# Moving feed-forward tiles between the front and the steps of a scan

## The chip, the cores and the metric

The kernel runs on one core of a Trainium2 chip. The metric is device time in microseconds for one execution, the median of several runs. Its engines are called by the profile's names: PE (TensorE, matmuls), DVE (VectorE), ACT (ScalarE), POOL (GpSimd) and SP (SyncE, which here issues nearly all DMAs). Everything is float32.

## What is computed

The input x is 4 sequences of 1024 rows with 512 columns. A block of three layers is applied, each with a residual: half a feed-forward layer (ffn), a selective-scan (Mamba) layer, half a feed-forward layer with the same weights. Cut to what matters:

```python
x = x + 0.5 * ffn(layernorm(x))            # stage 1
x = x + mamba(layernorm(x))
x = x + 0.5 * ffn(layernorm(x))            # stage 2

def ffn(x):                                # inner size 1408
    g = (x @ gate_w.T) * gate_s
    u = (x @ up_w.T) * up_s
    return ((silu(g) * u) @ down_w.T) * down_s

def mamba(x):                              # inner size 1024, 16 states, conv of 4 taps
    h, gate = split(W_in @ x)
    h = silu(causal_conv(h) + conv_b)
    ts, Bm, Cm = rms parts of Wx @ h       # 128 + 16 + 16
    delta = softplus(Wdt @ ts + dt_bias)
    s_t = exp(delta_t * A) * s_(t-1) + delta_t * B_t * h_t     # along the sequence
    y = (sum over states of s_t * C_t) + D * h
    return Wout @ (y * silu(gate))
```

## The kernel before

Rows are cut into 32 tiles of 128. A scan step covers 256 rows (two tiles), so there are 16 steps, `NCS`, four for each sequence. Within a step the scan goes over 8 blocks of 128 inner channels and 4 groups of states: 32 units (`unit`, L553). A unit makes exps on ACT (L569), products on POOL (L572), four scans on DVE (L576), products with C on DVE (L584). Two units later, PE adds the states up with a small matmul into `yps` (L594).

Beside the units, other work is spread over the step as a list of parts. Each part has a cost for PE and for DVE, and the loop at the end of the kernel takes a part off whenever the units' share of the cost has run ahead (`done`, `vector`), or when the parts up to `ready[k]` have to be through in the first 22 of the 32 units. The parts of one step k are:

- `prep_*`: for step k+1, load x1 (`prep_load`, L336), normalize and transpose (`flips`, L645; `prep_flip`), the h half of W_in and the conv (`prep_conv`, `hp`, L372 and L383), the product with Wx (`sp`, L407), its transposes (`t`), and the DMAs that spread B and C (`bc`). The last of these parts is `ready[k]`.
- `gate(k)` (L534, `gp`): the gate half of W_in for step k itself. `tail(k - 1)` (L612, `op`): Wout of the step before.
- `FFN(k, tiles)` (L239): a group of feed-forward tiles that share one pass over the weights. `gate()` has 11 parts of 4 matmuls with as many columns as the group has rows, `up()` the same, `down()` has one part for each tile, 11 matmuls of 512 columns (`fo`, L315). After gate parts 3, 7 and 10 an ACT silu follows, between two loads of activation tables (L195, L196). A tile is (1, r) for stage 1 or (2, r) for stage 2. A step can prepare rows only after stage 1 of them is done, and stage 2 needs x2, written two steps later.

The 64 tiles (32 in each stage) are divided thus: the group `start` in front, one group beside each step, the group `end` behind. Before the change `start` has 2 tiles, step 0 has 4, step 1 has 2, steps 2 to 13 have 4, steps 14 and 15 have 2, the end has 4.

`front` is a hand-written list that runs before the first unit: `start`'s three products, then ffn[0]'s flips, step 0's preparation, and `BEGUN` = 7 of the 11 gate parts of ffn[0]. Then come the head of the first two and of the next two blocks (`head`, delta: `dp`, L486, with ACT, POOL) and their DMAs (`rows`, `spread`). Step 0's own list is written out separately in `background`: the last four gate parts and the up parts woven with `gate(0)`, then down, flips and conv for step 1, and `params` of step 1 at the very end.

Weights go through a ring of 14 buffers; a program-ordered queue loads at most `LEAD` = 12 blocks ahead, and the down blocks are held until a group's last down part. A part that is put off (`defer`) is emitted after the next part with a cost. The tile framework then gives each engine its own order; instructions that are pinned keep the program's. [...]

Of the kernel before, what the change touches and what calls it, by code (L numbers as in the profile page):

```python
# [23 lines left out]
J = T // P  # L24
CPB = L // T
NCS = B * CPB
# [5 lines left out]
HEAD = 10  # L32
BEHIND = 2
LEAD = 12
BEGUN = 7
RING = 14


@with_exitstack
def macaron_kernel(ctx: ExitStack, tc: tile.TileContext, a: dict, out: bass.AP):  # L40
# [119 lines left out]
    def settle():  # L160
        while deferred:
            deferred.pop(0)[1]()
# [18 lines left out]
    NOTHING = Work(0, 0, lambda: None)  # L181

    def then(f, *args):
        return Work(0, 0, lambda: f(*args))
# [54 lines left out]
    class FFN:  # L239
# [35 lines left out]
        def gate(self):  # L275
            self.done = 0

            def part(it):
                def emit(w):
                    if it == 0:  # L280
                        self.hd = p1.tile([P, NF, 2 * T], F32, tag="hd", name=f"hd{self.name}")
                    gp = self.product("gate_w", it, w[0])
                    nc.scalar.activation(  # L283
                        self.hd[:, it, : self.n], gp, AF.Copy, scale=gate_s[:, it : it + 1]
                    )
                    if it % 4 == 3 or it == NF - 1:
# [350 lines left out]
    def weave(xs, by):  # L637

        r = []
        for n, w in enumerate(xs):  # L640
            r.append(w)
            r += by[n : n + 1]
        return r, by[len(xs) :]

    def flips(f, prep):  # L645

        seq = [(f, t) for t in range(len(f.tiles))] if f else []
        if prep is not None:
            seq += [(None, j) for j in range(J)]
        xn = {}  # L650

        def begin(n):
            if n < len(seq):
                of, t = seq[n]
                xn[n] = of.stats(t) if of else prep_stats(prep, t)

        def start():
            begin(0)
            begin(1)

        def part(n):
            def emit():
                of, t = seq[n]
                if of:
                    of.flip(xn[n], t)
                else:
                    prep_flip(prep, t, xn[n])
                begin(n + 2)

            return Work(KH * P, H if n + 2 < len(seq) else 0, emit)  # L670

        return [Work(0, 2 * H, start)] + [part(n) for n in range(len(seq))]

    first = [(1, r) for r in range(J, NCS * J)]
    second = [(2, r) for r in range((NCS - 1) * J)]
    beside = {}
    for k in range(NCS):
        ones = min(len(first), 4 if k == 0 else 2)  # L680
        twos = 2 if k >= 2 else 0
        beside[k] = [first.pop(0) for _ in range(ones)] + [second.pop(0) for _ in range(twos)]
        assert NCS * J - len(first) >= min(NCS, k + 3) * J
        assert all(r < (k - 1) * J for stage, r in beside[k] if stage == 2)
    last = second + [(2, r) for r in range((NCS - 1) * J, NCS * J)]
    ffn = {k: FFN(k, beside[k]) for k in range(NCS)}

    def end_load():
# [5 lines left out]
    def background(k):  # L694

        f = ffn[k]
        if k == 0:
            down, turn, params = f.down(), flips(None, 1), prep_params(1)
            ready[k] = params[-1]
            return (  # L700
                weave(gate_0[BEGUN:] + f.up(), gate(0))[0] + down[:J]
                + [then(prep_load, 1), turn[0]] + weave(down[J:], turn[1:])[0] + [then(ffn[1].load)]
                + weave(prep_conv(1), flips(ffn[1], None))[0] + [NOTHING] + params
            )
        prep = k + 1 if k + 1 < NCS else None
        gates, out_of = gate(k), tail(k - 1)
        turn = flips(None, prep) if prep is not None else []
        conv = params = []
        if prep is not None:
            conv, params = prep_conv(prep), prep_params(prep)  # L710
            ready[k] = params[-1]
        parts = [then(tail_load, k - 1)]
        if prep is not None:
            parts.append(then(prep_load, k + 1))
        parts += turn[:1]
        p = [NOTHING] * 4 + gates + turn[1:] + out_of + conv
        tiles = f.gate() + f.up()
        p = [p[n : n + 2] for n in range(0, len(p), 2)]
        p += [[NOTHING]] * 4 + [[w] for w in params]
        turn = flips(ffn[k + 1], None) if k + 1 < NCS else []  # L720
        for n, w in enumerate(tiles):
            parts.append(w)
            for q in p[n : n + 1]:
                parts += q
            if n == len(tiles) - NF and k + 1 < NCS:
                parts.append(then(ffn[k + 1].load))
            if n == len(tiles) - NF and k + 1 == NCS:
                parts.append(then(tail_load, k))
                parts.append(then(end_load))
            if n == len(tiles) - 2:  # L730
                parts += turn[:1]
        w, turn = weave(turn[1:2] + f.down(), [NOTHING] + turn[2:])
        return parts + w + turn

    ready = {}


    start = FFN("p", [(1, r) for r in range(J)])
    down, gate_0 = start.down(), ffn[0].gate()
    turn_f, turn_m = flips(ffn[0], None), flips(None, 0)  # L740
    front = flips(start, None) + start.gate() + [then(load_resident)] + start.up()
    front += [down[0], turn_f[0], down[1], then(prep_load, 0)] + turn_f[1:] + [gate_0[0], gate_0[1]]
    front += [turn_m[0], gate_0[2]] + turn_m[1:] + prep_conv(0)
    front += weave(gate_0[3:BEGUN], prep_params(0))[0]
    beside_scan = [background(k) for k in range(NCS)]
    end = FFN("e", last)
    turn = flips(end, None)
    back_end = tail(NCS - 1) + turn + end.gate() + end.up() + end.down()
    for w in front + [w for b in beside_scan for w in b] + back_end:
        if w.blocks:  # L750
            queue.append(w)

# [4 lines left out]
    for w in front:  # L757
        do(w)
    settle()
    chores = head(0, 0)  # L760
    while chores:
        chores.pop(0)()
    for i in range(2):
        rows(0, i)
        spread(0, i)
    chores = head(0, 2)
    while chores:
        chores.pop(0)()
    units = NI * NS


# [122 lines left out]
```

## Time and profile before

| what | value |
|---|---|
| median of 3 runs | 3323.13 us (3322.13 to 3327.34) |
| profiled execution, its own time | 3324.85 us |
| its span | 3323.0 us |
| granted TensorE clock, mean | 0.975 |
| PE / DVE / ACT / POOL busy | 3129.9 / 2441.5 / 1877.0 / 1952.8 us |
| bytes moved by DMA | 506.42 MB, mean 152 GB/s |

The page gives busy time by engine, then 40 slices of 83 us with the busy share in tenths, then DMA, the chain of work that ended last, and the costliest groups. A waiting engine's idle time is put down to the instruction that released it last. Stages are not marked in the profile; they are found by counting scans (128 to a step).

### The profile page before, as it was taken

Reading aid. Unit: us, or ns where it says so; the run is one execution under the profiler, and the core shown is the slowest. Engines: PE = TensorE matmul, PEld = TensorE weight load, DVE = VectorE, ACT = ScalarE, POOL = GpSimd, SP = SyncE. Lnnn points to the kernel's source line nnn. Section 1 sums busy time; section 2 is a strip of 40 time slices with the busy share of each in tenths; the row PEclk is TensorE's granted clock in tenths of the full one; section 3 lists DMA queues with packets and bytes.
Section 4 is the critical chain, followed back from the end, with each engine's and each line's share of the span. In section 5 each row is a group of like instructions: output and inputs, shape, how many; then the busy total and the mean of one; then the engine's idle time right before and its main releaser. Section 6 shows DMA issues by size and latency. Waiting matters only on the chain.

```text
span 3323.0 us, 41725 instructions
## 1 busy us (share of the span) xinstructions
PE 3129.9 (94%) x12448; PEld 1615.6 (49%) x12448; DVE 2441.5 (73%) x4213; ACT 1877.0 (56%) x4300; POOL 1952.8 (59%) x1895
## 2 busy tenths in 40 slices
PE   8897688999999999999999999999999999988799
PEld 6534353545445444544545454454545454554434
DVE  2176697887778778787968778786877878698831
ACT  3445565746576564756556475665647465666430
POOL 1255667566666657567665756666575666667520
PEclk9988798999999999999999999999999999999899
DMA  7335466556466565545656555656555564556521
GB/s 238 109 92 136 124 175 169 159 135 180 124 171 168 169 168 144 161 132 172 162 161 174 146 156 131 185 149 172 161 159 157 133 187 128 173 166 171 165 92 45
DMA packets 287425, 506.42 MB, mean 152 GB/s; under 512 B 32096, under 2 KB 50272, under 8 KB 287200
## 3 DMA queue, kind: packets, MB, share of 16 engines
q1 hardware_dynamic: 285616, 503.31, 54.2%
q8 instruction: 100, 1.64, 0.2%
q14 instruction: 125, 1.02, 0.1%
q10 hardware_dynamic: 1584, 0.45, 0.1%
HBM read 442.03 MB, written 61.60 MB: 152 GB/s over the span
## 4 chain that ended last, share of the span: by engine, by line
PE 68%; DVE 18%; ACT 7%; POOL 3%; issue 3%; DMA 1%; SPq 0%; ACTq 0%; DVEq 0%; POOLq 0%
PE fo L315 15%; PE gate_w L269 13%; DVE da L576 10%; PE up_w L269 8%; PE gp L541 6%; PE yps L594 6%; PE op L623 6%; PE hp L372 5%; DVE pr L584 4%; ACT da L569 2%; PE dp L486 1%; DVE hd L300 1%; PE gate_we L269 1%; POOL sb L572 1%; PE foe L315 1%
## 5 line engine op out<-in xcount | busy, mean ns | idle before, releaser
L572 POOL TENSOR_TENSOR sb<-rep,bc 128x512 f32<-128x512 f32 x1024 | 1284.7, 1274 | 804.3 <-DVE da L576 639.8
L576 DVE TENSOR_TENSOR_SCAN da<-da,state,sb 128x256 f32<-128x256 f32 x1536 | 1049.7, 737 | 199.9 <-ACT da L569 161.1
L569 ACT ACTIVATE da<-rep,a_w 128x256 f32<-128x256 f32 x2048 | 902.2, 473 | 268.7 <-DVE pr L584 253.5
L584 DVE TENSOR_TENSOR pr<-da,bc 128x512 f32<-128x512 f32 x1024 | 660.2, 676 | 90.6 <-ACT state L581 81.1
L269 PE MATMUL gate_w<-fxT,w_gate_w 128*128 128x512 f32 (+1 forms) x1408 | 592.4, 566 | 8.4 <-ACT g L545 3.5
L269 PE MATMUL up_w<-fxT,w_up_w 128*128 128x512 f32 (+1 forms) x1408 | 577.4, 561 | 4.4 <-PE hp L372 3.4
L315 PE MATMUL fo<-w_down_w,hd 128*128 128x512 f32 x1276 | 563.5, 597 | 0.0
L594 PE MATMUL yps<-pr,fold 128*32 128x256 f32 x4096 | 370.4, 399 | 109.1 <-DVE pr L584 102.6
L269 PEld LDWEIGHTS gate_w<-fxT,w_gate_w 128*128 128x128 f32 x1408 | 266.6, 194 | 272.6 <-issue 233.9
L581 ACT COPY state<-da 128x2 f32<-128x2 f32 x768 | 120.2, 164 | 492.0 <-DVE da L576 483.3
L269 PEld LDWEIGHTS up_w<-fxT,w_up_w 128*128 128x128 f32 x1408 | 263.3, 192 | 271.5 <-issue 231.8
L315 PEld LDWEIGHTS fo<-w_down_w,hd 128*128 128x128 f32 x1276 | 239.8, 192 | 283.9 <-issue 278.8
L576 DVE TENSOR_TENSOR_SCAN da<-da,sb 128x256 f32<-128x256 f32 x512 | 321.7, 679 | 61.3 <-ACT da L569 48.1
L594 PEld LDWEIGHTS yps<-pr,fold 128*32 128x32 f32 x4096 | 108.6, 110 | 403.0 <-DVE pr L584 176.7
L372 PE MATMUL hp<-mxT,w_W_in 128*128 128x259 f32 x1024 | 241.2, 388 | 6.7 <-issue 2.5
L541 PE MATMUL gp<-mxT,w_W_in 128*128 128x256 f32 x1024 | 246.0, 388 | 0.8 <-ACT g L545 0.5
L623 PE MATMUL op<-w_Wout,u 128*128 128x512 f32 x512 | 230.7, 600 | 6.3 <-POOL sb L572 2.6
L517 POOL TENSOR_SCALAR e<-z 128x512 f32<-128x512 f32 x64 | 124.4, 1943 | 175.9 <-ACT z L498 167.6
L383 DVE SCALAR_TENSOR_TENSOR u<-hp,conv_w,u 128x256 f32<-128x256 f32 x384 | 176.2, 474 | 66.0 <-ACT u L376 61.0
L372 PEld LDWEIGHTS hp<-mxT,w_W_in 128*128 128x128 f32 x1024 | 190.8, 190 | 59.8 <-issue 21.0
L541 PEld LDWEIGHTS gp<-mxT,w_W_in 128*128 128x128 f32 x1024 | 188.3, 190 | 61.6 <-issue 22.9
L283 ACT ACTIVATE hd<-gate_w,gate_s 128x512 f32<-128x512 f32 (+1 forms) x176 | 113.9, 648 | 137.1 <-PE gate_w L269 136.9
(112 smaller groups left out, 2592.9 us busy)
## 6 DMA issues: line engine op xcount, KB each, us to landing
rep<-row SPq DMA_DIRECT2D x512, 256.0 KB, 5.4
w_W_in<-in_W_in_dram SPq DMA_DIRECT2D x256, 256.0 KB, 3.2
w_gate_w<-in_gate_w_dram SPq DMA_DIRECT2D x198, 256.0 KB, 4.0
w_up_w<-in_up_w_dram SPq DMA_DIRECT2D x198, 256.0 KB, 3.5
w_down_w<-down_w SPq DMA_DIRECT2D x187, 256.0 KB, 3.0
row<-dd SPq DMA_DIRECT2D x128, 256.0 KB, 3.0
w_Wout<-in_Wout_dram SPq DMA_DIRECT2D x128, 256.0 KB, 3.1
bc<-bcd SPq DMA_DIRECT2D x64, 256.0 KB, 5.3
```

The lines of the kernel that those rows point to most:

```text
L269: nc.tensor.matmul(o[:, : self.n], lhsT=w[:, k, :], rhs=self.xT[:, k, : self.n], start=(k == 0), stop=(k == KH - 1),)
L315: nc.tensor.matmul(op, lhsT=self.hd[:, it, t * P : (t + 1) * P], rhs=wd[it], start=(it == 0), stop=(it == NF - 1),)
L372: nc.tensor.matmul(hp[:, : K - 1 + T], lhsT=w[:, kk, :], rhs=st[k]["xnT"][:, kk, :], start=(kk == 0), stop=(kk == KH - 1),)
L383: pin(nc.vector.scalar_tensor_tensor(u[:, i, :], hp[:, q : q + T], conv_w[:, i, q : q + 1], u[:, i, :], ALU.mult, ALU.add,))
L517: lambda: pin(nc.gpsimd.tensor_scalar(e, z, 1.0, 1.0, ALU.add, ALU.subtract)),
L541: nc.tensor.matmul(gp[:, :T], lhsT=w[:, kk, :], rhs=st[k]["xnT"][:, kk, K - 1 :], start=(kk == 0), stop=(kk == KH - 1),)
L569: nc.scalar.activation(da[:, j, :], rep[:, h + j, 0, :], AF.Exp, scale=a_w[:, b0 + h + j, g : g + 1])
L572: nc.gpsimd.tensor_tensor(sb, rep[:, hs, 1, :], d["bc"][:, g : g + 1, :].to_broadcast([P, 2, T]), ALU.mult)
L576: nc.vector.tensor_tensor_scan(da[:, j, :], da[:, j, :], sb[:, j, :], 0.0 if first else state[:, b0 + h + j, g : g + 1], ALU.mult, ALU.add,)
L584: nc.vector.tensor_tensor(pr[:, hs, :], da, d["bc"][:, NS + g : NS + g + 1, :].to_broadcast([P, 2, T]), ALU.mult)
L594: nc.tensor.matmul(yp[j * Q : (j + 1) * Q, :], lhsT=fold, rhs=pr[:, j, :], start=(g == 0), stop=(g == NS - 1),)
L623: nc.tensor.matmul(op, lhsT=st[k]["u"][:, i, j * P : (j + 1) * P], rhs=wo[i], start=(i == 0), stop=(i == NI - 1),)
```

## The change

- `start` takes four stage-1 tiles in place of two. Its four down parts: two, then step 0's preparation begins (`prep_load(0)` and flips), the third down part and the fourth lie among them. ffn[0]'s flips are woven into the conv of step 0.
- ffn[0] has three tiles. Four of its gate parts (`FRONT`) lie in front, two between the first and the second head, five behind the second head.
- A table `BESIDE` gives each step's stage-1 and stage-2 tiles: steps 0, 1, 4, 7, 10, 13, 14 and 15 have three, steps 2, 3, 5, 6, 8, 9, 11 and 12 have four. The end keeps four.
- Step 0's list is built by the same code as the others' (without gate parts, Wout of an earlier step, and the four empty places in front): flips, `gate(0)`, conv and `params` for step 1 are woven with the up parts, and down comes last, with the flips of ffn[1].

```diff
-BEGUN = 7
+FRONT = 4
+BESIDE = [(3, 0), (3, 0), (2, 2), (2, 2), (1, 2), (2, 2), (2, 2), (2, 1), (2, 2), (2, 2), (2, 1), (2, 2), (2, 2), (1, 2), (0, 3), (0, 3)]
...
-    first = [(1, r) for r in range(J, NCS * J)]
-    second = [(2, r) for r in range((NCS - 1) * J)]
+    first = [(1, r) for r in range(2 * J, NCS * J)]
+    second = [(2, r) for r in range((NCS - 2) * J)]
...
-        ones = min(len(first), 4 if k == 0 else 2)
-        twos = 2 if k >= 2 else 0
+        ones, twos = BESIDE[k]
...
-    last = second + [(2, r) for r in range((NCS - 1) * J, NCS * J)]
+    last = [(2, r) for r in range((NCS - 2) * J, NCS * J)]
...
-        if k == 0:
-            down, turn, params = f.down(), flips(None, 1), prep_params(1)
-            ready[k] = params[-1]
-            return (
-                weave(gate_0[BEGUN:] + f.up(), gate(0))[0] + down[:J]
-                + [then(prep_load, 1), turn[0]] + weave(down[J:], turn[1:])[0] + [then(ffn[1].load)]
-                + weave(prep_conv(1), flips(ffn[1], None))[0] + [NOTHING] + params
-            )
...
-        parts = [then(tail_load, k - 1)]
+        parts = [then(tail_load, k - 1)] if k else []
...
-        p = [NOTHING] * 4 + gates + turn[1:] + out_of + conv
-        tiles = f.gate() + f.up()
+        p = [NOTHING] * (4 if k else 0) + gates + turn[1:] + out_of + conv
+        tiles = (f.gate() if k else []) + f.up()
...
+        for q in p[len(tiles):]:
+            parts += q
...
-    start = FFN("p", [(1, r) for r in range(J)])
+    start = FFN("p", [(1, r) for r in range(2 * J)])
...
-    front += [down[0], turn_f[0], down[1], then(prep_load, 0)] + turn_f[1:] + [gate_0[0], gate_0[1]]
-    front += [turn_m[0], gate_0[2]] + turn_m[1:] + prep_conv(0)
-    front += weave(gate_0[3:BEGUN], prep_params(0))[0]
+    front += [down[0], down[1], then(prep_load, 0), turn_m[0], down[2]] + turn_m[1:]
+    front += [turn_f[0]] + weave(prep_conv(0), [down[3]] + turn_f[1:])[0]
+    front += weave(gate_0[:FRONT], prep_params(0))[0]
...
+    between = gate_0[FRONT:]
...
+    for w in between[:2]:
+        do(w)
     chores = head(0, 2)
     while chores:
         chores.pop(0)()
+    for w in between[2:]:
+        do(w)
```

More of the change, by code (lines that the diff above doesn't have):

```diff
@@ L684, in macaron_kernel @@
         assert all(r < (k - 1) * J for stage, r in beside[k] if stage == 2)
-    last = second + [(2, r) for r in range((NCS - 1) * J, NCS * J)]
+    assert not first and not second
+    last = [(2, r) for r in range((NCS - 2) * J, NCS * J)]
     ffn = {k: FFN(k, beside[k]) for k in range(NCS)}
@@ L696, in background @@
         f = ffn[k]
-        if k == 0:
-            down, turn, params = f.down(), flips(None, 1), prep_params(1)
-            ready[k] = params[-1]
-            return (
-                weave(gate_0[BEGUN:] + f.up(), gate(0))[0] + down[:J]
-                + [then(prep_load, 1), turn[0]] + weave(down[J:], turn[1:])[0] + [then(ffn[1].load)]
-                + weave(prep_conv(1), flips(ffn[1], None))[0] + [NOTHING] + params
-            )
         prep = k + 1 if k + 1 < NCS else None
-        gates, out_of = gate(k), tail(k - 1)
+        gates, out_of = gate(k), tail(k - 1) if k else []
         turn = flips(None, prep) if prep is not None else []
@@ L748, in macaron_kernel @@
     back_end = tail(NCS - 1) + turn + end.gate() + end.up() + end.down()
-    for w in front + [w for b in beside_scan for w in b] + back_end:
+    for w in front + gate_0[FRONT:] + [w for b in beside_scan for w in b] + back_end:
         if w.blocks:
```

## The prediction

> **What bounds the kernel now.** I read the page from the top first. TensorE (PE) is the busy engine, in nearly every slice:
>
> ```profile
> PE 3129.9 (94%) x12448; PEld 1615.6 (49%) x12448; DVE 2441.5 (73%) x4213; ACT 1877.0 (56%) x4300; POOL 1952.8 (59%) x1895
> ...
> PE   8897688999999999999999999999999999988799
> ...
> PEclk9988798999999999999999999999999999999899
> ```
>
> The first slices and the ones near the end are the holes. So I cut the span into the stages of the program. A step makes 128 scans, so every 128th scan is a border: first scans at 169.7, 371.8, 547.3 and so on. The view by windows (length, then busy us of PE, PEld, DVE, ACT, POOL, then the clock):
>
> ```profile
> 0.00:169.70 169.70, 143.77 (x509) 96.07 (x510) 35.83 (x79) 67.97 (x104) 30.78 (x53) 0.97 0.57 174
> 169.70:371.80 202.10, 162.97 (x661) 84.68 (x659) 144.59 (x255) 101.34 (x267) 106.68 (x101) 0.89 0.43 115
> 371.80:547.30 175.50, 135.66 (x620) 76.01 (x620) 148.56 (x260) 104.56 (x268) 124.68 (x121) 0.87 0.56 160
> 547.30:740.50 193.20, 187.23 (x715) 93.62 (x716) 151.49 (x261) 115.54 (x276) 122.03 (x119) 0.98 0.54 146
> 931.10:1119.60 188.50, 187.00 (x752) 93.88 (x751) 146.37 (x263) 116.32 (x281) 123.67 (x120) 1.00 0.57 157
> 1119.60:1314.60 195.00, 192.18 (x763) 96.16 (x762) 153.51 (x262) 117.54 (x283) 121.01 (x117) 1.00 0.57 160
> 2847.90:3029.90 182.00, 157.95 (x764) 95.69 (x763) 147.20 (x257) 112.89 (x286) 121.34 (x114) 0.93 0.64 182
> 3029.90:3188.70 158.80, 134.88 (x576) 71.14 (x574) 131.87 (x217) 82.07 (x168) 101.37 (x86) 0.92 0.51 151
> ```
>
> Rows in order: front, steps 0, 1, 2, 4, 5, 14, 15. Steps 2 to 13 carry four feed-forward tiles each, take 188.5 to 195.0 us (mean 191.9), and PE lacks only 1.5 to 6 us: they are PE-bound. Steps 1, 14 and 15 carry two tiles and PE idles 24 to 40 us, but they last 175.5, 182.0 and 158.8 (step 15 prepares no next step). They are held by VectorE (DVE) and what it waits for: length minus DVE busy is 27.0, 34.8 and 26.9, mean 29.6. In PE-bound steps the same difference is about 40 (195.0 - 153.5 = 41.5; 188.5 - 146.4 = 42.1).
>
> What a tile costs on PE is read where PE runs undisturbed, in the chain in order of time (88 records are 44 matmuls, two records each):
>
> ```profile
> 12.00 21.32 PE gate_wp L269 x88
> 33.33 18.99 PE up_wp L269 x88
> 52.32 18.88 PE fop L315 x44
> ...
> 3243.69 37.77 PE up_we L269 x88
> 3281.45 37.78 PE foe L315 x88
> ```
>
> A matmul of 512 columns takes 37.77/44 = 0.858 us, one of 256 takes 18.99/44 = 0.43: time goes with columns. One tile (128 columns in 88 gate and up matmuls, 11 down matmuls of 512) is 88 x 0.2145 + 11 x 0.858 = 28.3 us, in whatever group it sits. Before and after there are 18 groups (front, 16 steps, end), so weight loads, silu calls and DMA bytes stay; nothing is saved by size. A four-tile step needs 189 us of PE, a three-tile one 161, a two-tile one 132.
>
> **Front: +31 us.** Tiles 2 to 4, so 56.6 us more PE. But ffn[0] shrinks from four tiles to three, and its eleven gate parts, all before the first scan in both orders, go from 11 x 3.55 (39 us) to 11 x 2.6 (28.6). Step by step: two more normalized tiles ahead of the first matmul cost about 2 (ACT 0.81 + 0.58 each, partly overlapped), so it starts at 14. Gate, up and down of four tiles at end-stage prices are 38.5 + 38.2 + 37.8 = 114.5 (the 256-column gate of before ran at 0.485 instead of 0.43, and that loss goes). Then flips of the next step 2.2, hp 14.3 (before's own 89.67 to 103.8), three ffn[0] flips 2, the wait for silu of u 5.5, sp + gate part + sp 7.2, two gate parts 5.2, transposes to dp about 2: 38.4, so dp at 167, where before had it at 134.85. The silu wait was 8.5 because a silu of hd stood ahead of u's on ACT; the new order puts u's first.
>
> From dp to the first scan before took 34.8, and it ended on PE, not on the rep transfer:
>
> ```profile
> 134.85 1.97 PE L486 MATMUL dp<-tsT,w_dt 128*128 128x256 f32 x8 [0.61 <-DVE tsT L451]
> 169.00 0.75 DVE L300 SCALAR_TENSOR_TENSOR hd<-up_w,up_s,hd 128x512 f32<-128x512 f32 x1 [4.41 <-PE up_w L269]
> 169.67 1.27 DVE L576 TENSOR_TENSOR_SCAN da<-da,sb 128x256 f32<-128x256 f32 x2
> ```
>
> DVE's scan stood behind an hd multiply that waited for up_w. The new order keeps that: ahead of the first scan PE has two dp, seven gate parts, two up parts and three gp: 1.8 + 18.2 + 5.2 + 5.3 = 30.5, and ACT has the third gp copy and then the exps, about 1. With PE stalls of 2.4, as before at 143.12 and 149.78: 167 + 34 = 201. SP issues row and rep of tiles 0 and 1 ahead of later weights, so they land in the shadow of this. Two new waits in the front: fo of the fourth tile holds the eleven down blocks of 14 ring buffers, so W_in loads for hp 3 on follow it (3.2 us to land; they start 9 us earlier: nothing); hp 1 waits for it on PE (counted). First scan at 201, +31.3; I allow +27 to +40.
>
> **Step 0: -28 us.** 202.1 is DVE 144.6 and 57.5 idle. What goes: the 9.9 us wait at the border for bc of step 1; most of 15.0 us in which DVE waited for fo; 2.9 for xi (windowed timeline, 250.64 and 252.50), since x1 rows 2 and 3 now come from the front; about 2 of hd.
>
> ```profile
> POOL sb L572 <- DMA bc<-bcd: 20.1, 1, 20.1
> DVE xf L323 <- PE fo L315: 15.0, 4, 6.2
> DVE da L576 <- POOL sb L572: 11.8, 3, 9.9
> ```
>
> The bc chain was last in step 0; the new order emits conv and params before down, and PE's order shows sp and t beside units 4 and 5 of 8. PE has only 28 (up) + 28 (down) + 59 (gp, hp, yps, sp, dp, flips) = 115 us, no bound. DVE 143 (nine hd multiplies 0.16 shorter, one xf less, one stats more) + idle 57.5 - 26.8 = 30.7: 173.7. The xf waits shrink to about 3: two-tile steps show none.
>
> **Three-tile steps: the term that decides.** DVE busy is known: 3.4 less than in a four-tile step (11 hd multiplies at 0.58 for 0.745, one xf 0.68, one stats 0.85), 2.8 more than with two tiles. Its idle is not shown for three tiles. It lies between 29.6 (two) and 40 (four). PE needs 161 of some 182, so it stops being the bound and I take the value nearer to two tiles: 32.5, and keep 25.4 (step 1 less its 1.6 of bc wait) and 40 for the range. What is late next is ACT: the three hd silus, g's and u's block the exps (a table load 1.28, the silu, a load 1.28), and step 14 shows two such waits of 7.2 and 9.2 us at two tiles.
> - Steps 4, 7, 10, 13 lose a tile: 188.5, 191.0, 192.9, 193.5 become 143.0, 150.3, 149.8, 148.6 plus 32.5: 175.5, 182.8, 182.3, 181.1. Together -44.2.
> - Step 1 gains one: 150.4 + 32.5 = 182.9, +7.4 (its start no longer carries stalled work done early in step 0).
> - Step 14: 150.0 + 32.5 = 182.5, +0.5.
> - Step 15: 133.9 + 29.5 = 163.4, +4.6; PE needs 138.
>
> Four-tile steps keep their length: step 2 follows a step with spare PE and still took 193.2. The end, the same four tiles, keeps 134.3. SP sees the same blocks; xi of a next step asks for at most the same store as before, and in steps 1 to 13 for one row earlier, so no queue is moved past a later store.
>
> **Sum:** +31.3 - 28.4 - 44.2 + 7.4 + 0.5 + 4.6 = -28.8. The profiled execution has span 3323.0 and its own time 3324.85, the median is 3323.13, so I subtract from the median: 3294.
>
> [...] In two-tile steps the granted clock falls: 0.87, 0.93, 0.92 against 1.00. The change puts some PE idle into four more steps. [...] At 0.93, PE's 161 become 173, still under 182; at 0.87 they become 185, 2.5 us over, about 15 in six steps. [...] I take 0.93, as three tiles leave fewer gaps than two.
>
> **Rivals.**
> 1. Slower: the three-tile step stays at the pace of a four-tile one, because ACT, PE and DVE wait for each other in turn (PE's yps for pr, ACT's hd for gate_w, DVE's scan for the exp). For: four-tile idle 40 while step 14 has 34.8 with half the tiles. Against: step 15 has 26.9 and step 1 27.0. Price: idle 40 adds 7.5 x 6 = 45, so 3339. It decides from an idle of 32.5 + 28.8/6 = 37.3 on.
> 2. Better: DVE idle as in step 1, 25.4, since PE is no longer asked for all its time: -43, 3251.
> 3. The change doesn't shorten step 0: DVE waits for fo as before (15) because flips, fo and yps interleave, or the front ends at +40. Either alone +9 to +12: 3304; with idle at 36 it is no change.
>
> **How the numbers follow.** Less than a 0.2% change (6.6 us) is about what a measurement of this kernel can't tell from none. Main case, idle 29 to 36: 0.47, of it 0.45 faster, 0.02 same. Rival 2: 0.15, faster. Rival 1: 0.25, slower mostly, 0.03 same. Rival 3 with idle near 36: 0.13, of it 0.02 faster, 0.08 same, 0.03 slower. So faster 0.62, same 0.13, slower 0.25. Range: rival 2's 3251 and rival 1's 3339 are its ends, rounded to 3254 and 3340, with 2 in 10 outside.
>
> **What would show it.** After the change: first scan near 201; no bc wait at the step 0 to 1 border; step 0 near 174; steps 1, 4, 7, 10, 13, 14 at 176 to 183 with DVE idle about 32; PEclk there above 0.93. Three-tile steps over 187, or a first scan past 210, would prove it wrong.

## The result, and the profile after

The changed kernel takes 3304.23 us, the median of four runs (3302.43 to 3307.95); the kernel before took 3324.42 beside it. The ratio is 0.9941 with an interval of 0.9926 to 0.9956: about 20 us faster. The forecast was 3294, so the sign is right, the range holds the time, and about a third of the forecast gain is missing. The profiled execution of the changed kernel is its slowest of the four, 3307.95 with a span of 3306.2; stage sums below are made against that span, which is 16.8 shorter than the 3323.0 of before.

The first part of the page, and the rows of PE and of its clock in 40 slices:

```profile
PE 3139.3 (95%) x12448; PEld 1612.0 (49%) x12448; DVE 2435.9 (74%) x4213; ACT 1879.9 (57%) x4299; POOL 1949.8 (59%) x1895
...
PE   8988898999999999999989999999999999999999
...
PEclk9988999999999999999999999999999999999999
```

The totals hardly move, as they should: the same work was put elsewhere. The hole near the end of before (slices 36 to 38) is gone; what is left of the first hole is mostly step 0. The view by windows, cut again at every 128th scan; columns are bounds and length, busy time of PE, PEld, DVE, ACT and POOL, then clock, DMA share and GB/s:

```profile
0.00:199.90 199.90, 183.44 (x536) 98.73 (x536) 40.99 (x83) 69.33 (x101) 31.77 (x56) 1.00 0.46 140
199.90:368.20 168.30, 134.30 (x579) 70.97 (x580) 139.41 (x254) 96.71 (x261) 112.64 (x107) 0.86 0.50 141
368.20:556.90 188.70, 171.06 (x726) 90.93 (x724) 151.39 (x262) 115.27 (x282) 120.16 (x118) 0.97 0.59 162
556.90:750.40 193.50, 187.43 (x714) 93.60 (x715) 151.69 (x260) 115.75 (x276) 121.31 (x119) 0.98 0.51 142
940.40:1122.20 181.80, 173.31 (x780) 94.81 (x778) 144.89 (x264) 117.14 (x290) 122.38 (x118) 0.98 0.65 180
1122.20:1314.60 192.40, 186.42 (x714) 93.31 (x715) 151.61 (x260) 115.50 (x276) 120.05 (x118) 0.98 0.53 146
2820.60:3008.80 188.20, 173.25 (x732) 92.16 (x731) 150.17 (x260) 115.19 (x282) 120.59 (x116) 0.96 0.58 159
3008.80:3171.30 162.50, 154.24 (x596) 72.91 (x595) 133.67 (x219) 82.31 (x164) 100.99 (x86) 0.97 0.51 150
```

These are the front and steps 0, 1, 2, 4, 5, 14 and 15, as before. All stages, in us:

| stage | before | forecast | after | change forecast | change measured |
|---|---|---|---|---|---|
| front | 169.7 | 201 | 199.9 | +31.3 | +30.2 |
| step 0 | 202.1 | 173.7 | 168.3 | -28.4 | -33.8 |
| step 1 | 175.5 | 182.9 | 188.7 | +7.4 | +13.3 |
| steps 4, 7, 10, 13 | 765.9 | 721.7 | 737.3 | -44.2 | -28.6 |
| step 14 | 182.0 | 182.5 | 188.2 | +0.5 | +6.2 |
| step 15 | 158.8 | 163.4 | 162.5 | +4.6 | +3.7 |
| eight steps of four tiles | 1534.7 | as before | 1526.4 | 0 | -8.3 |
| end | 134.3 | 134.3 | 134.9 | 0 | +0.6 |
| sum | 3323.0 | | 3306.2 | -28.8 | -16.7 |

The last column adds to 16.7 and the spans differ by 16.8; that is rounding.

What the front's four tiles cost on PE is read from the chain in order of time, whose rows are start, length and group:

```profile
14.76 40.80 PE gate_wp L271 x88
55.56 37.77 PE up_wp L271 x88
93.32 28.32 PE fop L317 x66
...
125.29 9.44 PE fop L317 x22
```

Gate, up and down take 40.8 + 37.8 + 37.8 = 116.3 against 114.5 forecast: at four tiles the front runs at the price of the end stage (37.8 each), except that the gate took 3.0 more, of which 0.7 were forecast. The timeline of the front's end (start, length, instruction, and in brackets the idle time before it and what ended that):

```profile
167.81 1.10 PE L488 MATMUL dp<-tsT,w_dt 128*128 128x256 f32 x4 [0.61 <-DVE tsT L453]
196.49 0.62 DVE L302 SCALAR_TENSOR_TENSOR hd<-up_w,up_s,hd 128x384 f32<-128x384 f32 x1 [5.35 <-PE up_w L271]
199.87 2.44 DVE L578 TENSOR_TENSOR_SCAN da<-da,sb 128x256 f32<-128x256 f32 x4 [2.76 <-ACT da L571]
```

dp comes at 167.8 (167 forecast) and the first scan at 199.9 (201). Only the last releaser is another one: the scan waited 2.76 for ACT's exp, not for the hd multiply before it, which was done 2.8 earlier.

The view of waits in step 0 (who waited for whom, us in all, times, longest) has no wait for bc any more, and none of DVE for fo:

```profile
DVE u L602 <- PE yps L596: 10.7, 3, 8.3
POOL sb L574 <- DVE xf L325: 7.3, 1, 7.3
DVE pr L586 <- ACT state L583: 6.8, 11, 2.6
...
DVE da L578 <- ACT da L571: 4.6, 3, 2.8
```

Before, DVE lost 15.0 to fo and POOL 20.1 to bc, 9.9 of which DVE lost again. DVE's idle time, length less busy, falls from 57.5 to 28.9. In step 7, which carries three tiles, the same view shows what DVE waits for now:

```profile
DVE da L578 <- ACT da L571: 15.4, 7, 4.1
DVE u L602 <- PE yps L596: 12.1, 4, 5.5
...
DVE hd L302 <- PE up_w L271: 4.3, 3, 3.3
```

Before, with four tiles, the first lines of the same step were these:

```profile
DVE da L576 <- ACT da L569: 17.6, 8, 6.5
DVE xf L323 <- PE fo L315: 8.9, 2, 7.1
DVE u L600 <- PE yps L594: 4.4, 4, 2.0
```

The exps are the largest item, before and after, and no item holds the 36.0 us of idle alone. With one tile less the wait for fo is gone; in its place came longer waits for yps and for up_w, which are results of PE too. DVE idle in the six three-tile steps is 37.3, 36.9, 36.0, 32.8, 32.0 and 38.0 (steps 1, 4, 7, 10, 13, 14), mean 35.5.

### The profile page after: what moved, and what is told of

Read it like the earlier page. It is cut to its first block, busy times and chain, and to the rows that moved or that the text cites. A ratio compares the mean times of both kernels' runs of the same rounds, so it can differ in the third digit from the quotient of the medians.

```text
span 3306.2 us, 41606 instructions
## 1 busy us (share of the span) xinstructions
PE 3139.3 (95%) x12448; PEld 1612.0 (49%) x12448; DVE 2435.9 (74%) x4213; ACT 1879.9 (57%) x4299; POOL 1949.8 (59%) x1895
## 4 chain that ended last, share of the span: by engine, by line
PE 66%; DVE 19%; ACT 8%; issue 3%; POOL 2%; DMA 1%; SPq 0%; DVEq 0%; ACTq 0%; POOLq 0%
PE fo L317 13%; PE gate_w L271 13%; DVE da L578 11%; PE up_w L271 8%; PE gp L543 6%; PE yps L596 6%; PE op L625 5%; PE hp L374 4%; DVE pr L586 4%; ACT da L571 2%; PE dp L488 1%; DVE u L385 1%; PE gate_wp L271 1%; PE gate_we L271 1%; PE foe L317 1%
## 5 line engine op out<-in xcount | busy, mean ns | idle before, releaser
L571 ACT ACTIVATE da<-rep,a_w 128x256 f32<-128x256 f32 x2048 | 906.9, 475 | 296.5 <-DVE pr L586 280.5
L271 PE MATMUL gate_w<-fxT,w_gate_w 128*128 128x384 f32 (+1 forms) x1408 | 579.4, 558 | 17.4 <-ACT hd L285 12.2
L271 PE MATMUL up_w<-fxT,w_up_w 128*128 128x384 f32 (+1 forms) x1408 | 564.0, 549 | 6.3 <-PE hp L374 2.3
L317 PE MATMUL fo<-w_down_w,hd 128*128 128x512 f32 x1232 | 544.3, 595 | 3.0 <-ACT fxT L236 3.0
L317 PEld LDWEIGHTS fo<-w_down_w,hd 128*128 128x128 f32 x1232 | 228.8, 190 | 276.3 <-issue 267.0
L543 PEld LDWEIGHTS gp<-mxT,w_W_in 128*128 128x128 f32 x1024 | 188.3, 191 | 67.6 <-issue 20.2
L374 PEld LDWEIGHTS hp<-mxT,w_W_in 128*128 128x128 f32 x1024 | 191.3, 191 | 58.9 <-issue 18.0
L285 ACT ACTIVATE hd<-gate_w,gate_s 128x384 f32<-128x384 f32 (+1 forms) x176 | 111.5, 636 | 97.9 <-PE gate_w L271 97.2
```

The costliest lines, as they stand in the source:

```text
L271: nc.tensor.matmul(o[:, : self.n], lhsT=w[:, k, :], rhs=self.xT[:, k, : self.n], start=(k == 0), stop=(k == KH - 1),)
L317: nc.tensor.matmul(op, lhsT=self.hd[:, it, t * P : (t + 1) * P], rhs=wd[it], start=(it == 0), stop=(it == NF - 1),)
L374: nc.tensor.matmul(hp[:, : K - 1 + T], lhsT=w[:, kk, :], rhs=st[k]["xnT"][:, kk, :], start=(kk == 0), stop=(kk == KH - 1),)
L543: nc.tensor.matmul(gp[:, :T], lhsT=w[:, kk, :], rhs=st[k]["xnT"][:, kk, K - 1 :], start=(kk == 0), stop=(kk == KH - 1),)
L571: nc.scalar.activation(da[:, j, :], rep[:, h + j, 0, :], AF.Exp, scale=a_w[:, b0 + h + j, g : g + 1])
```

## The experiments

Two questions were open. Which part of the change brings the gain: the order of step 0 or the spreading of tiles? And what holds a three-tile step at 185.7 (the mean of the six) when PE has been relieved of a tile? For the second there were several accounts, and from "Two tiles where there are three" on the expectations letter them. One is the prediction's own: ACT's silus, and the table loads around them, keep the exps back, and PE is no bound (A). Against it stand PE itself (B), the wait of u for yps (C), ACT's state copies (E), and no single engine at all, but a chain through DVE and the short exchanges between engines (D). In the first three experiments A is another theory, spelled out there.

One caution goes for all of them: an edit of one line lets the framework plan a new order of instructions on every engine, and steps change by a few us with it: in the run with two tiles, of the steps that keep theirs, step 14 changed by -6.0 and the eight four-tile steps by -3.0 to +1.6. A difference of 2 or 3 us in one step shows little; one of 10 or more, or one of the same sign in all six steps, can be read. Except where another kernel is named, edits are to the changed kernel.

### Step 0 in its old order

```diff
+        if k == 0:
+            down, turn, params = f.down(), flips(None, 1), prep_params(1)
+            ready[k] = params[-1]
+            woven, rest = weave(down[J:], turn[1:])
+            return (
+                weave(f.up(), gate(0))[0] + down[:J]
+                + [then(prep_load, 1), turn[0]] + woven + rest + [then(ffn[1].load)]
+                + weave(prep_conv(1), flips(ffn[1], None))[0] + [NOTHING] + params
+            )
```

> The changed kernel with one part undone: step 0's list in its old order (up woven with gate, then down, then flips, conv and params for step 1 last), front and distribution as changed. Theory A (the order of step 0 is what paid for the front): step 0 goes from 168 to about 190 and the wait for bc at its end comes back (about 10 us), so about +25 us, 3329, or no gain left. Rival (step 0 is short only because it has less matmul work): step 0 stays below 173, within 5 us of the changed kernel's 3304.

Measured: 3323.09 us, ratio to the kernel before 0.9999 (0.999 to 1.0007). The whole gain is gone. Its step 0 by windows:

```profile
198.50:386.80 188.30, 146.21 (x649) 81.53 (x650) 139.73 (x254) 106.10 (x273) 107.63 (x104) 0.88 0.47 134
```

and two of the waits in it:

```profile
POOL sb L574 <- DMA bc<-bcd: 13.8, 1, 13.8
...
DVE hd L302 <- PE up_w L271: 13.0, 4, 4.5
```

Step 0 is 188.3 instead of 168.3 at the same DVE work (139.7 and 139.4): 20 us more of DVE idle, and the bc wait is back. So the order is worth 20 of step 0's 33.8; the other 14 (202.1 - 188.3) come with what moved to the front. But the order has to be paid for: step 0 can only be ordered like the others because x1 rows 2 and 3 come from the front.

### The spread alone, in the kernel before

```diff
+BESIDE = [(4, 0), (3, 0), (2, 2), (2, 2), (1, 2), (2, 2), (2, 2), (2, 1), (2, 2), (2, 2), (2, 1), (2, 2), (2, 2), (2, 2), (0, 3), (0, 3)]
...
-        ones = min(len(first), 4 if k == 0 else 2)
-        twos = 2 if k >= 2 else 0
+        ones, twos = BESIDE[k]
```

> The kernel before with the distribution alone: front of two tiles and step 0 of four as before, then three tiles in steps 1, 4, 7, 10, 14, 15, four in the others. Theory A (a three-tile step takes 182 to 189, hardly less than a four-tile step, and 6 to 13 more than a two-tile one): what steps 4, 7, 10 and the steps after them save (18 to 25 us), steps 1, 14, 15 pay back (about 20), so 3318 to 3324. Rival (evening out is the gain): -15 us or more, below 3309.

Measured: 3314.52 us, ratio 0.9971 (0.996 to 0.9982), 9 us faster than before, half of what the whole change brings. The windows of steps 0 and 1:

```profile
168.80:376.00 207.20, 168.71 (x665) 86.24 (x663) 143.92 (x257) 106.03 (x271) 107.77 (x104) 0.90 0.41 112
376.00:562.50 186.50, 154.79 (x642) 78.36 (x642) 151.30 (x260) 106.72 (x268) 125.22 (x121) 0.89 0.56 156
```

Step 0, which this edit leaves at four tiles in the old order, took 5 more than before, and step 1 pays 11 for its third tile, step 15 3.7, step 14 nothing (182.0); steps 4, 7 and 10 fall to 180.7, 188.0 and 184.6, by 7.8, 3.0 and 8.3. Both theories missed: the rival wanted under 3309, the other 3318 or more.

### Front and order alone, no spread

```diff
-BESIDE = [(3, 0), (3, 0), (2, 2), (2, 2), (1, 2), (2, 2), (2, 2), (2, 1), (2, 2), (2, 2), (2, 1), (2, 2), (2, 2), (1, 2), (0, 3), (0, 3)]
+BESIDE = [(4, 0), (2, 0), (2, 2), (2, 2), (2, 2), (2, 2), (2, 2), (2, 2), (2, 2), (2, 2), (2, 2), (2, 2), (2, 2), (0, 2), (0, 2), (0, 2)]
```

> The changed kernel with the distribution uneven again: front of four and step 0 in the new order, step 0 with four tiles, step 1 with two, steps 2 to 12 with four, 13 to 15 with two. Theory A (even or uneven matters little): steps 4, 7, 10, 11 get 6 us each longer, steps 1, 13, 14, 15 shorter by 5 to 10 each, step 0 some 5 longer: 3300 to 3312. Rival (evening out is the gain): 3320 or more.

Measured: 3330.2 us, ratio 1.0017 (1.001 to 1.0024): slower than before, and 26 slower than the changed kernel. Theory A had not expected that; the rival, 3320 or more, came true. Steps 0 and 1:

```profile
203.30:378.80 175.50, 148.92 (x614) 73.84 (x613) 140.86 (x254) 95.96 (x261) 111.75 (x104) 0.93 0.47 133
378.80:564.90 186.10, 155.25 (x704) 93.57 (x702) 148.50 (x261) 114.76 (x284) 120.74 (x119) 0.88 0.58 163
```

Two things are to be seen. Step 0 in the new order with four tiles takes 175.5: 26.6 less than before, which does not pay for a front of 203.3 (+33.6). And step 1 with two tiles takes 186.1, where before's took 175.5 with two, at the same DVE work (148.5). So the idle of 27.0, on which the prediction rested, belongs to that one step of before. A possible reason lies in the traces: there a part of step 1's gate products had been done in step 0. The gate products of the feed-forward group by window (length, PE busy and records, then clock, DMA share and GB/s), in steps 0, 1 and 14 of before:

```profile
169.70:371.80 202.10, 12.09 (x40) 0.89 0.43 115
371.80:547.30 175.50, 14.24 (x48) 0.87 0.56 160
2847.90:3029.90 182.00, 26.77 (x102) 0.93 0.64 182
```

A group's gate has 88 records; before's step 1 did 48 of them, this kernel's 80. ACT has 104.6 us of work in the one and 114.8 in the other. Whether this is all of the difference in idle was not tested.

Set beside the changed kernel, these spans tell the price of a tile by place. A third tile on top of two costs 2.6 in step 1, 3.1 in 13, 4.0 in 14, 3.7 in 15. A fourth taken away saves 7.2 in step 0, 6.7 in 4, 3.0 in 7, 8.1 in 10. The front is 3.4 shorter, because ffn[0] is smaller by a tile. That is 13.4 paid and 28.4 saved, 15.0 of the 22.1 us between the two spans; 5.0 more come in step 11, which keeps its four tiles, and the rest is smaller than the changes of order.

So front and order alone cost 6, the spread alone brings 9, and both bring 20. They don't add. With the new front and the spread but the old order, the front uses up all that the spread brings (the first experiment, 3323); with front and order but no spread, the kernel is slower than before. The spread pays alone; the front and the order pay only together, and beside the spread.

### Two tiles where there are three

```diff
-BESIDE = [(3, 0), (3, 0), (2, 2), (2, 2), (1, 2), (2, 2), (2, 2), (2, 1), (2, 2), (2, 2), (2, 1), (2, 2), (2, 2), (1, 2), (0, 3), (0, 3)]
+BESIDE = [(3, 0), (3, 0), (2, 2), (2, 2), (1, 1), (2, 2), (2, 2), (2, 0), (2, 2), (2, 2), (2, 0), (2, 2), (2, 2), (1, 1), (0, 3), (0, 3)]
...
+    more_end = FFN("x", second)
+    back_end += [then(more_end.load)] + flips(more_end, None) + more_end.gate() + more_end.up() + more_end.down()
```

The four tiles taken out make a second group at the end, so only the steps are read, not the total.

> The changed kernel with only two tiles in steps 4, 7, 10 and 13; the four tiles left over go into a second group of four behind the end (about 115 us more there). Read are the lengths of the four steps, 181.7, 188.0, 184.6 and 183.0 in the changed kernel (mean 184.3). Theory A (the length is VectorE's busy time plus ScalarE's table loads and silus, which are the same for two and three tiles): only VectorE's 2.8 us less, mean 181. Rival B (the load of TensorE still sets the waits): the 28 us less of matmuls take 8 us or more off, mean 176 or less. Total 3405 or 3389.

Measured: 3413.09 us in one run. Steps 4, 7, 10, 13 take 180.1, 175.7, 184.8 and 183.5, mean 181.0, against 184.3. Steps 7 and 10 by windows:

```profile
1503.40:1679.10 175.70, 154.02 (x758) 92.84 (x756) 148.92 (x261) 106.34 (x224) 120.65 (x118) 0.93 0.64 184
...
2062.20:2247.00 184.80, 158.06 (x758) 94.13 (x756) 149.39 (x261) 114.81 (x289) 121.65 (x119) 0.92 0.61 177
```

and a line of the waits in step 7:

```profile
DVE da L578 <- ACT da L571: 16.6, 4, 8.0
```

The mean hides two cases. Steps 4, 10 and 13 change by -1.6, +0.2 and +0.5 us for the 28 us of PE work that a tile is: there PE's load is not what holds a three-tile step. Step 7 loses 12.3, more than rival B asked. It is the one of the four without state copies (the last step of a sequence makes none); whether that is the reason no run shows. So theory A's mean of 181 came out, but not as A said it would, by 2.8 in each step.

DVE idle is 38.0, 26.8, 35.4 and 34.7. The view of waits tells what it is made of. Summed over steps 4, 7, 10 and 13, in us:

| DVE waits | four tiles (before) | three (changed) | two (this run) |
|---|---|---|---|
| scans for exps (ACT) | 57.3 | 46.6 | 67.3 |
| u for yps (PE) | 18.1 | 36.5 | 19.0 |
| hd for up_w (PE) | 0.7 | 13.8 | 20.7 |
| xf for fo (PE) | 33.1 | 0 | 0 |
| all idle | 160.5 | 137.6 | 134.9 |

The first tile taken away ends the waits for fo, 33.1, and the waits for yps and up_w take nearly all of it back (+31.5). The second ends half of the waits for yps, and those for exps grow by about as much. A wait that goes makes room for others.

The step length says more here than PE's busy row. In these four steps that row falls from 189 to 175 to 157 on average as tiles are taken away, by 14 and 18 for 28 us of work each. The clock differs too, 0.92 to 0.93 in the two-tile steps and 0.97 to 0.99 in the three-tile ones (in the changed kernel's step 0, a yps matmul took 0.63 us in a stretch at half speed; in its step 3, at a mean clock of 1.00, 0.38); how much of the difference that makes was not looked into.

### Fewer and more silu calls

A silu of hd covers up to four gate parts, with a table load before and after it. Here it covers up to six, and up to two:

```diff
-                    if it % 4 == 3 or it == NF - 1:
+                    if it % 6 == 5 or it == NF - 1:
```

> The changed kernel with two silus of hd in a group (after gate parts 5 and 10) in place of three (3, 7, 10): one pair of table loads, 2.56 us of ScalarE, less in each step. Theory A (blocks of ScalarE by silu and its table loads set a three-tile step's idle): three-tile steps 3 us shorter, four-tile steps the same, about -20 us: 3284. Rival B (TensorE's lateness sets it): within 5 us of 3304.

```diff
-                    if it % 4 == 3 or it == NF - 1:
+                    if it % 2 == 1 or it == NF - 1:
```

> The changed kernel with six silus of hd in a group (after parts 1, 3, 5, 7, 9, 10) in place of three: three more pairs of table loads, 7.7 us of ScalarE more in each step, in shorter blocks. Theory A: three-tile steps 5 to 8 us longer, four-tile steps less, +40 us or more: 3345. Rival B: under +15 us: 3319 or less. A third outcome would be a gain, if it is the length of one block and not the sum that counts.

Measured: 3377.83 us, ratio 1.0158 (1.014 to 1.0177), with fewer calls; 3344.74, ratio 1.0061 (1.0045 to 1.0077), with more. Both are slower. Fewer calls remove 35 table loads but make three-tile steps longer, 191.1 on average, and four-tile steps too, 194.1 for 190.8: in the three-tile steps DVE waits 11 to 20 us for yps (mean 16.1) instead of 7 to 12 (mean 9.4). That both theories missed. More calls put 7.7 us of work on ACT in a step (six table loads of 1283 ns). The whole is 40 us longer, as theory A said, but not in the way it said: three-tile steps are 2.1 longer and not 5 to 8, four-tile steps 2.6, and step 15 with the end 7. So the number of table loads alone does not set the length. The size and the place of a block of silus seem to count as well; this edit changes both with the number, so it can't tell them apart.

### The u multiply one unit later

DVE waits for yps before u becomes u D + y. Here the program gives that instruction one unit later, when yps should be long there:

```diff
+    late = []
...
+        while late:
+            late.pop(0)()
...
-            nc.vector.scalar_tensor_tensor(u, u, d_w[:, i : i + 1], yp, ALU.mult, ALU.add)
+            def skip():
+                nc.vector.scalar_tensor_tensor(u, u, d_w[:, i : i + 1], yp, ALU.mult, ALU.add)
+
+            late.append(skip)
```

> The changed kernel with the multiply-add of u and D (VectorE, which waits for yps, 7 to 12 us in a three-tile step) written one unit later. Theory A: this wait only stands in for another, VectorE goes on to wait for exps: within 6 us of 3304. Rival C (the wait for yps is a cost of its own): up to 8 us off each step that isn't bound by TensorE, -40 us: 3264.

Measured: 3315.19 us, ratio 0.9973 (0.996 to 0.9986), so 11 slower than the changed kernel; three-tile steps 185.3. The wait of u for yps is still there, 11.9 us in step 7 for 12.1. But the edit did not do what was meant. The instruction is not pinned, and by the trace it stands at the same place in DVE's order, counted in scans before it, in 100 of 128 cases, among them every one that waits. So this is no test of rival C.

### State copies: left out, and on VectorE

ACT copies the last columns of the scans, two at a time, into `state`, 64 times in a step, in between the exps. The last step of each sequence (3, 7, 11, 15) has no copies. First the copies are left out, the state being zero throughout:

```diff
+    nc.gpsimd.memset(state, 0.0)
...
-            if not last:
-                nc.scalar.copy(state[:, b0 + h : b0 + h + 2, g : g + 1], da[:, :, T - 1 : T])
```

> The changed kernel without ScalarE's copies of the last state (64 in each step, 10.5 us, in 12 of 16 steps; each waits for a scan of VectorE, and VectorE's product waits for it); the state that a block of rows starts from stays zero. The output is not the reference's. Three-tile steps 1, 4, 10, 13, 14 have the copies now, steps 7 and 15 haven't. Theory E (the copy's hand-over between VectorE and ScalarE is the largest part of the idle): these five lose 6 us or more each, step 7 stays at 188. Theory D: under 3 us.

Measured: 3303.01 us in one run, as the changed kernel. Three-tile steps are 189.5, four-tile steps 187.9 (185.7 and 190.8 in the changed kernel). The five three-tile steps that had copies lose 6 to 7 us of ACT work and are 4.9 us longer on average, which neither theory expected; step 7, which had none, is 1.7 shorter. In the six, DVE's waits for copies, 5.4 us on average, are gone; the waits for exps (13.2 to 16.3) and for yps (9.4 to 12.8) grow by more. Then the same copies on DVE:

```diff
-                nc.scalar.copy(state[:, b0 + h : b0 + h + 2, g : g + 1], da[:, :, T - 1 : T])
+                nc.vector.tensor_copy(state[:, b0 + h : b0 + h + 2, g : g + 1], da[:, :, T - 1 : T])
```

> The changed kernel with the copies of the last state on VectorE in place of ScalarE. VectorE gets 64 copies of 128 x 2 in each of 12 steps, 0.06 to 0.16 us each, 4 to 10 us; ScalarE loses 10.5 us and a wait for VectorE. Theory E: saves more than it costs, three-tile steps 3 us shorter, 3285 to 3300. Theory D: VectorE's busy time comes on top in three-tile steps (4 to 10 us in five steps), nothing in four-tile ones: 3320 to 3350.

Measured: 3316.08 us, ratio 0.998 (0.997 to 0.9989), 12 slower than the changed kernel, with three-tile steps of 191.3 and four-tile steps of 188.4. DVE has about 4 us more to do in a step with copies, and three-tile steps are 5.6 longer, four-tile steps 2.4 shorter; neither range was met. That DVE's own work counts in three-tile steps fits; but leaving the copies out lengthened them by 3.8 too, so part of the 5.6 is a new order and not DVE.

### No silu tables

Silu is replaced by the identity, so that ACT needs no silu table. The kernel then computes something else; the work on the other engines is the same.

```diff
-        pin(nc.scalar.activation(t, t, AF.Silu))
-        pin(nc.scalar.preload_act_table_set("natural_log_exp_and_others"))
+        pin(nc.scalar.activation(t, t, AF.Identity))
```

> The changed kernel with the silus left out: the same ScalarE instruction on the same tile as Identity, without the two table loads around it (12.8 us of ScalarE less in a full step). The output is not the reference's. Read are steps 1, 4, 7, 10, 13, 14 (three tiles, mean 185.7, VectorE idle 35.5). Theory A (blocks of ScalarE by table loads): they lose 8 us or more each, mean under 178. Theory D (a chain of short waits round VectorE, ScalarE and TensorE, no one of which is the cause): 3 us or less, mean over 182. Four-tile steps stay near 191 in both.

Measured: 3363.75 us in one run, 60 slower than the changed kernel, and no test of the question. ACT's groups show why:

```profile
L500 ACT ACT_TABLE_LOAD x64 | 82.1, 1283 | 1.7
L570 ACT ACT_TABLE_LOAD x63 | 80.8, 1283 | 1.7 <-DMA rep<-row 0.6
```

The removed preload had also given exp and ln one table set. Without it ACT loads a table before the ln of every head pair and another before the exp that follows. The changed kernel's rows, for comparison:

```profile
L197 ACT ACT_TABLE_LOAD x86 | 110.3, 1283 | 1.5
L198 ACT ACT_TABLE_LOAD x86 | 110.3, 1283 | 1.5
```

So the same edit again, with that set loaded once at the start:

```diff
+    pin(nc.scalar.preload_act_table_set("natural_log_exp_and_others"))
```

> The changed kernel with the silus left out as in e1_no_tables, but with the table set of exp and ln loaded once at the start, so that one table load is left in the whole program (e1_no_tables turned out to have 129, as many in a step as it was meant to remove, between exp and ln of each head). The output is not the reference's. Theory A (blocks of ScalarE by table loads set the idle of a three-tile step): the six three-tile steps go from a mean of 185.7 to under 178, the whole to under 3270. Theory D (a chain of short waits, each covered by the next): over 182, the whole over 3285.

Measured: 3277.61 us, ratio to the kernel before 0.986 (0.9843 to 0.9876). One table load is left:

```profile
L750 ACT ACT_TABLE_LOAD x1 | 1.3, 1283 | 7.3 <-DMA a_w<-in_A_dram 7.3
```

Steps 7 and 10 by windows:

```profile
1493.70:1677.50 183.80, 172.11 (x776) 94.00 (x774) 151.39 (x263) 98.41 (x217) 124.16 (x121) 0.98 0.64 177
...
2059.60:2239.70 180.10, 172.62 (x776) 93.68 (x774) 151.33 (x262) 104.68 (x279) 122.38 (x119) 0.99 0.66 181
```

ACT has 230 us less to do in all, 14 in step 1, and the kernel is 26.6 shorter. Three-tile steps take 181.9 instead of 185.7 (from 7.7 shorter in step 1 to 0.1 longer in step 4), their DVE idle 32.2 instead of 35.5. Table loads, and with them all that silu costs beyond an identity, are 3.3 of the 35.5 us. The result lies between what the two theories asked (under 178, over 182), next to the one that gives the loads no great part. It prices a cost and is not a version to use.

### A buffer more for the exps, one less for other products

To see whether DVE would wait less if the exps could run further ahead of the scans, a PSUM buffer was moved from the pool of all other matmul results (`ps_m`) to that of the exps (`ps_a`):

```diff
-    ps_a = ctx.enter_context(tc.tile_pool(name="ps_a", bufs=4, space=PSUM))
+    ps_a = ctx.enter_context(tc.tile_pool(name="ps_a", bufs=5, space=PSUM))
...
-    ps_m = ctx.enter_context(tc.tile_pool(name="ps_m", bufs=3, space=PSUM))
+    ps_m = ctx.enter_context(tc.tile_pool(name="ps_m", bufs=2, space=PSUM))
```

> The changed kernel with one bank of PSUM moved: five buffers for the exps that ScalarE makes ahead of the scans in place of four, two for all other matmuls in place of three. Theory A or E (ScalarE is late with exps): the waits of VectorE for exps (10 to 17 us in a three-tile step) fall by a third or more. But TensorE loses a buffer, and four-tile steps, bound by it, get longer: 3310 to 3360. Theory D: no fewer waits for exps.

Measured: 3624.8 us, ratio 1.0907 (1.0891 to 1.0923). From step 1 on the steps are about 209, some 20 more than in the changed kernel, whatever their tiles. A line of the waits in step 7:

```profile
DVE u L602 <- PE yps L596: 26.8, 4, 12.8
```

In the six three-tile steps the waits for exps fall from 13.2 to 9.7 us on average, by 27%, less than theory A or E asked; those for yps rise from 9.4 to 27.7, 18 of the 23 us by which these steps got longer. The third ps_m buffer is worth more than all that was studied here.

## Why the prediction was right, and where its sizes were off

Right, by its steps:

- The front. +30.2 for +31.3, with the parts where they were put: 116.3 of gate, up and down for 114.5, dp at 167.8 for 167, first scan at 199.9 for 201. Only the last wait before the scan was for ACT's exp and not for the hd multiply.
- Step 0. The bc wait and DVE's waits for fo went, as written. The step is 168.3 for 173.7. The term that was off is the idle taken away, 28.6 (57.5 less 28.9) where 26.8 was counted, and DVE's work, 139.4 where 143 was counted. By the first experiment 20 of the 33.8 are the order itself.
- The clock. Priced at 0.93 in three-tile steps from the trace of before; it shows 0.96 to 0.99 there, so PE had more room than was counted. The clock of 0.87, which would have cost 15, stayed in step 0 (0.86), where PE is no bound.
- The end and step 15 held within 1 us.

Mis-sized: the three-tile steps, "the term that decides". Their idle was put at 32.5 and came out at 35.5, 3.0 in each of six steps, 18 in all; their DVE work is 1.5 higher than read from before, 9 in all. Together that is the 27 us by which steps 1, 4, 7, 10, 13 and 14 miss their sum (+13.3 + 6.2 - 28.6 = -9.1 for -36.3). The 3.4 us less of DVE work for a tile was right, but only half of it lies in the step itself: steps 4 and 5 together have 3.4 less (299.9 to 296.5), and of these 1.9 show in step 5. At 37.3 the prediction's first rival would have taken over; its mechanism, a step that stays at the pace of a four-tile one, is about half of what happened: 35.5 lies nearer the four-tile steps' 40 than the 29.6 of two.

The reading that failed is the average of 29.6, made from steps 1, 14 and 15 of before. Step 15 prepares no next step, and step 1 had only 48 of its 88 gate records to do, which its row (x620 for x764 in step 14) could have told: with two tiles but a new step 0 it showed 37.6 (186.1 - 148.5), and in the middle of the kernel two tiles showed 26.8 to 38.0. No idle can be read off by the number of tiles alone.

"PE stops being the bound" was right as to PE's load: a second tile less changed three of four steps by 1.6 us or less. "What is late next is ACT" was not. Waits for exps are the largest item, but they were so with four tiles already and fell with the tile (57.3 to 46.6 over four steps). What took back the freed 33.1 was DVE waiting for single results of PE, yps and up_w (+31.5). ACT came next only with the second tile taken away (46.6 to 67.3). So, by the view of waits, DVE goes on waiting for PE in a three-tile step, though PE's load is no bound there.

That the range holds the time is in part luck. Two things that the prediction had not counted made up for 13.7 of the 27 us. Four-tile steps were costed at no change and lost 8.3, of it 5.0 in step 11; steps 5 and 8 follow a three-tile step as step 11 does and changed by -2.5 and +0.8, so why it was step 11 is open. And step 0 gave 5.4 more.

What holds a three-tile step is only settled in parts. Shown: not PE's load in three steps of four (step 7 is open), and not mainly the table loads (3.3 of 35.5). Neither edit of the state copies helped. Work taken from ACT, 6 to 7 us with the copies and about 14 with the tables, made three-tile steps 4.9 longer and 3.8 shorter. The rest lies in many waits, for exps, for yps, for hd, each mostly under 6 us. Three times a wait that was taken away came back as others: fo as yps and up_w, yps as exps, the copies as exps and yps. That they are a chain of exchanges between DVE, ACT and PE fits this; it is argued, not shown, and the wait for yps has not been tested by itself.

## What to carry to other kernels

Price moved work at the place where it lands: two tiles lengthened the front by 30 to 34 us, one cost mostly 3 to 4 in a step with two (11 in step 1 of the kernel before), and gave back 3 to 8 from a step with four, so taking work from full steps to half-empty ones paid here, and taking it to a stage that PE bounds paid only through the order that it made possible. Look at what the last stage of preparation waits for: here the inputs of step 1 were made last in step 0, and making their rows one stage earlier let 20 us of idle go. And do not read the idle of a relieved step from a special step such as the first or the last; count first whether its window holds all of its work. When an edit is meant to move an instruction, look in the trace whether it moved.

## What the runs showed of the hardware that was not expected

- What a table load cost depended on where it stood. 174 loads fewer (223 us of ACT time at 1283 ns), with the silus made identities, made the kernel 26.6 us faster, 12% of their time; 128 loads between ln and exp, 164 us, made it 86 us slower (3363.75, one run, and 3277.61, the two identity kernels), half of their time. The first kind stands around the silus, the second ahead of the exps that scans wait for; that this is why is argued, not shown.
- Moving one of three PSUM buffers from the pool `ps_m` to that of the exps cost about 20 us a step; in the three-tile steps most of it is DVE's waiting for yps (9.4 to 27.7 us).
- The granted clock fell to 0.86 in step 0 of the changed kernel, where PE idled 34 us of 168 in 21 gaps, the longest 3.5, 3.6 and 4.2. Step 4, with 8.5 us of idle in ten gaps, the longest 2.2, kept 0.98. In step 0 the clock's record is at full or at half speed: six stretches at half speed, 3.4 to 17 us long and 47 us of the step in all, are the 0.86. They outlast the gaps that they stand at: the longest, 17.0, begins in a gap of 5.35 (3.6 of it in the step), two of 10.2 stand at gaps of 4.2 and 3.5, and one of 3.4 begins at 276.4 after gaps of no more than 1.75 us. Two of the six (columns as in the table by windows, the clock third from the end):

```profile
201.30:218.30 17.00, 9.74 (x38) 3.69 (x39) 15.57 (x27) 8.13 (x25) 10.20 (x9) 0.50 0.87 274
...
276.40:279.80 3.40, 3.40 (x6) 1.69 (x5) 3.14 (x6) 2.28 (x7) 1.26 (x2) 0.50 0.00 0
```
